# Cross-attention with a quantised feed-forward on one core: feed-forward clamps on GpSimd, roundings and transposes spread over each unit, finer extremes, small blocks at both ends, padding zeroed by VectorE

## The chip, the cores and the metric

The kernel runs on one core of one Trainium2 chip. The metric is the device time in microseconds, the median of several runs; lower is better. Profiles are one execution each, taken by the hardware profiler. In them PE is TensorE, DVE is VectorE, ACT is ScalarE, POOL is GpSimd and SP is SyncE, which here only issues DMAs.

## The reference

The inputs are x (32 x 100 x 256), a context (32 x 361 x 256) and one mask, all float32. The output is x after two residual steps.

```
x = x + attention(layernorm(x), ctx, ctx, WQ, WK, WV, WO, mask)    # 16 heads of 64
x = x + ffn(layernorm(x), W1, b1, W2, b2)                          # 256 -> 1024 -> 256

def affine_quantize(x):
    scale = max((max(x) - min(x)) / 255, 1e-8)       # over the whole tensor
    zp = clip(round(-min(x) / scale) - 128, -128, 127)
    q = clip(round(x / scale) + zp, -128, 127)

def qlinear(x, W, b):
    xq, sx, zx = affine_quantize(x)
    wq, sw = sym_quantize(W)
    return einsum("bsh,oh->bso", xq - zx, wq) * (sx * sw) + b

ffn(x) = qlinear(gelu(qlinear(x, W1, b1)), W2, b2)
```

What matters for the order of work is that each of the two quantised layers needs the largest and the smallest value of its whole input before its first element can be rounded. So there are two points at which everything must be known: the normalised x of all 3200 rows before the first layer, and all 3200 x 1024 GELU outputs before the second.

## The kernel before

*Attention* goes through the 32 batches in turn. For each it makes scores of 16 heads, exponentials on ScalarE, transposed weights, the product with the values, and keys and values of the next batch. The order on TensorE is written out by hand there; in the feed-forward a scheduler orders TensorE by priority and data, and `follow(a, b)` pins an instruction behind another on one engine.

At the start the context is loaded into three buffers `c`, whose columns 361 to 384 are padding that must be zero (L170 to L171, on GpSimd). The values of batch 0 (`v_part`, L276) read this padding in their third slice. After them TensorE transposes the normalised x of the first group (`ln1_T`, L325), which waits for `ln1` (L309, VectorE), and that for the inverse deviations (L299, L300, GpSimd). GpSimd also builds the identity there, loads two biases (L582, L583) and copies a constant (L541).

`residual` (L515) adds each batch's attention output, keeps running extremes, and `keep` (L122) writes the row with the second bias to a DRAM buffer `xb2`, from which the feed-forward reads it back into 128-row blocks. `normalize` (L129) makes the normalised x in place.

*Feed-forward, first layer.* The eight groups of four batches (400 rows each) are rounded to int16 (`ix`), clamped into bf16 (`xq`), transposed on TensorE (`turn`, L746) and copied by ScalarE (`xqT`, L749). `round_rows` (L722) does rounding and clamp through `to_integers` (L699), whose two parts are

```
done = nc.vector.tensor_scalar(i, src, r, None, ALU.mult)   # L705, or on ScalarE, L707
return nc.vector.tensor_scalar(dst, i, lo, hi, ALU.max, ALU.min)   # L710
```

The groups form units of 1, 1, 2, 2 and 2 groups. A unit has eight slices `fc` of the hidden width; for each TensorE multiplies (L781) and ScalarE applies GELU (L788) into `h`. VectorE takes the maximum and minimum of `h` over `spans` of slices (L794, L795): 2, 2, 4 in the first unit, 4 and 4 in the others. The groups of the next unit are rounded and turned together at the third slice of the unit before it.

`affine_params` (L99) reduces the extremes over the partitions on GpSimd (L107) and makes scale, inverse scale `rs`, zero point and bounds on VectorE (L109 to L119).

*Second layer.* The 25 blocks of 128 rows are grouped into `blocks` of 1, 3, 4, 4, 4, 4, 4 and 1. Each block is rounded in two halves (`ih`, ScalarE or VectorE), clamped by VectorE (`hq`), multiplied (L824), scaled and added to the kept row (`ot`, L831), and written (L834). The final sum of a block stands on VectorE just behind its clamps.

`warm` (L141) puts idle matmuls where TensorE would stand still.

Of the kernel before, what the change touches and what calls it, by code (L numbers as in the profile page):

```python
# [8 lines left out]
F32 = mybir.dt.float32  # L9
BF16 = mybir.dt.bfloat16  # L10
# [10 lines left out]
MAGIC = 12582912.0  # L21
# [6 lines left out]
def kernel(  # L28
# [66 lines left out]
    def follow(a, b):  # L95

        tc.add_manual_dep(a.ins, b.ins.name, ORDER)

    def affine_params(ext, name, weight):  # L99

        def col(n):
            return const.tile([P, 1], F32, tag=f"{n}{name}", name=f"{n}{name}")

        al = const.tile([P, 2], F32, tag=f"al{name}", name=f"al{name}")
        nc.gpsimd.partition_all_reduce(al, ext, P, bass_isa.ReduceOp.max)  # L107
        sc, rs, z, lo, hi = col("sc"), col("rs"), col("z"), col("lo"), col("hi")
        nc.vector.tensor_tensor(sc, al[:, 0:1], al[:, 1:2], ALU.add)  # L109
        nc.vector.tensor_scalar(sc, sc, 1.0 / 255.0, 1e-8, ALU.mult, ALU.max)  # L110
        nc.vector.reciprocal(rs, sc)


        nc.vector.tensor_scalar(z, al[:, 1:2], rs, MAGIC, ALU.mult, ALU.add)
        nc.vector.tensor_scalar(z, z, MAGIC, 0.0, ALU.subtract, ALU.max)
        nc.vector.tensor_scalar(lo, z, QMAX - QMIN, -1.0, ALU.min, ALU.mult)
        known = nc.vector.tensor_scalar(hi, lo, QMAX - QMIN, None, ALU.add)
        c = col("c")
        follow(nc.vector.tensor_tensor(c, sc, weight, ALU.mult), known)  # L119
        return rs, lo, hi, c, known, al  # L120

    def keep(b, adder, queue):  # L122

# [2 lines left out]
        queue.dma_start(out=xb2[b], in_=t)  # L126
        return i

    def normalize(b, after):  # L129

        xb = xg[b // G][:, b % G, :]
        i = nc.vector.tensor_scalar(
            xb, xb, mv2[:, b, 0:1], rstd2[:, b : b + 1], ALU.subtract, ALU.mult
        )
        follow(i, after)
# [5 lines left out]
    def warm(ps, n, gate=None):  # L141

        if gate is not None:
            nc.tensor.matmul(ps[: gate.shape[1], : gate.shape[1]], gate, gate, start=True, stop=True)
        for _ in range(n):
            nc.tensor.matmul(ps, idle[:, :P], idle, start=True, stop=True)


    with ExitStack() as att:
# [17 lines left out]
        NCB = 3  # L167
        cbuf = [wpool.tile([P, NDC, SP], F32, tag=f"c{i}", name=f"c{i}") for i in range(NCB)]
        pb = wpool.tile([TP, 2 * NHP, SP], F32, tag="p", name="p")
        for t in cbuf + [pb]:  # L170
            nc.gpsimd.memset(t[:, :, S:SP], 0.0)  # L171

        qbuf = [
            wpool.tile([P, PAIRS, G, 2, RH], F32, tag=f"q{q}", name=f"q{q}") for q in range(NQ)
# [501 lines left out]
    N = B * T  # L676
    h = hpool.tile([P, NFC, N], F32, tag="h", name="h")

    sizes = [1, 3] + [G] * ((N // P - 5) // G) + [1]
    blocks = [(sum(sizes[:i]), n) for i, n in enumerate(sizes)]  # L680
    assert sum(sizes) == N // P and len(blocks) == NG


    ext1 = const.tile([P, 2], F32, tag="ext1", name="ext1")
    with tc.high_priority():
        nc.vector.memset(ext1, -BIG)
        for r, op, neg, col in ((rmax, ALU.max, False, 0), (rmin, ALU.min, True, 1)):
            nc.vector.tensor_tensor(r, r, mv2[:, :, 0], ALU.subtract)
            nc.vector.tensor_tensor(r, r, rstd2, ALU.mult)
            found = nc.vector.tensor_reduce(ext1[:T, col : col + 1], r, AX.X, op, negate=neg)  # L690
        rx, lox, hix, c1, known, alx = affine_params(ext1, "x", scales["1"][1])
    warm(ps_h.tile([P, 512], F32, tag="ph", name="warm2"), 7, alx)

    def rows(dram, first, n):

        r = dram.rearrange("b t d -> (b t) d")[first * P : (first + n) * P]
        return r.rearrange("(c p) d -> p c d", p=P)

    def to_integers(pool, dst, src, r, lo, hi, tag, on_vector, after=None):  # L699

        i = pool.tile(list(src.shape), I16, tag=f"i{tag}", name=f"i{tag}") if tag[0] == "x" else (
            pool.tile([P, NF2, G * P], I16, tag=f"i{tag}", name=f"i{tag}")[:, :, : src.shape[2]]
        )
        if on_vector:
            done = nc.vector.tensor_scalar(i, src, r, None, ALU.mult)  # L705
        else:
            done = nc.scalar.activation(i, src, AF.Copy, bias=0.0, scale=r)  # L707
        if after is not None:
            follow(done, after)
        return nc.vector.tensor_scalar(dst, i, lo, hi, ALU.max, ALU.min)  # L710

    identb = const.tile([P, P], BF16, tag="identb", name="identb")
    nc.vector.tensor_copy(identb, ident)
# [2 lines left out]
    units = [(0, 1), (1, 1)] + [(g, 2) for g in range(2, NG, 2)]  # L716
    xqTs = {}
    gelu = None

    xqs = {}  # L720

    def round_rows(g, part, parts, on_vector, after):  # L722

        if part == 0:
            xqs[g] = f1.tile([T, G * D], BF16, tag="xq", name=f"xq{g}", bufs=4)
        src = xg[g].rearrange("t b d -> t (b d)")
        n = G // parts
        sl = slice(part * n * D, (part + 1) * n * D)
        done = to_integers(
            f1, xqs[g][:, sl], src[:, sl], rx[:T], lox[:T], hix[:T], f"x{n}", on_vector, after  # L730
        )
        if part == parts - 1 and g < len(blocks):

            nc.sync.dma_start(out=xf[g][:, : blocks[g][1], :], in_=rows(xb2, *blocks[g]))
        return done

    def turn(g, part, parts):

# [19 lines left out]
    k = 0  # L758


    done = round_rows(0, 0, 2, False, None)
    done = round_rows(0, 1, 2, True, done)
    for part in range(2):
        turn(0, part, 2)
    done = round_rows(1, 0, 1, True, done)
    follow(keep(B - 1, nc.vector, nc.sync), done)
    round_rows(2, 0, 1, True, done)
    for u, (g, n) in enumerate(units):
        ts = slice(g * GT, (g + n) * GT)
        spans = (2, 2, 4) if u == 0 else (4, 4)  # L770
        ends = [sum(spans[: i + 1]) for i in range(len(spans))]
        for fc in range(NFC):
            if fc == 2 and u + 1 < len(units):
                for i in range(*units[u + 1][:1], sum(units[u + 1])):
                    if i > 3:
                        round_rows(i, 0, 1, False, gelu)
                    turn(i, 0, 1)
            ph = ps_h.tile([P, 2, 512], F32, tag="ph", name=f"ph{u}_{fc}")
            for i in range(n):
                for dc in range(NDC):  # L780
                    nc.tensor.matmul(  # L781
                        ph[:, i, :GT],
                        w1qt[:, dc, fc * P : (fc + 1) * P],
                        xqTs[g + i][:, dc, :],
                        start=(dc == 0),
                        stop=(dc == NDC - 1),
                    )
            gelu = nc.scalar.activation(  # L788
                h[:, fc, ts].rearrange("p (k t) -> p k t", k=n), ph[:, :n, :GT],
                AF.Gelu, bias=b1t[:, fc : fc + 1], scale=c1,  # L790
            )
            if fc + 1 in ends:
                src = h[:, fc + 1 - spans[ends.index(fc + 1)] : fc + 1, ts]
                nc.vector.tensor_reduce(hmax[:, k : k + 1], src, AX.XY, ALU.max)  # L794
                done = nc.vector.tensor_reduce(hmin[:, k : k + 1], src, AX.XY, ALU.min)  # L795
                k += 1
                if k == 1:
                    round_rows(3, 0, 1, True, done)
        if u == 0:
            normalize(B - 1, done)  # L800

    ext2 = const.tile([P, 2], F32, tag="ext2", name="ext2")
    with tc.high_priority():
        nc.vector.tensor_reduce(ext2[:, 0:1], hmax[:, :k], AX.X, ALU.max)
        nc.vector.tensor_reduce(ext2[:, 1:2], hmin[:, :k], AX.X, ALU.min, negate=True)
        rh, loh, hih, c2, known, _ = affine_params(ext2, "h", scales["2"][1])
    warm(ps_h.tile([P, 512], F32, tag="ph", name="warm3"), 18, hmax[:, k - 1 : k])

    ff1.close()
    f2 = ctx.enter_context(tc.tile_pool(name="f2", bufs=2))  # L810
    for i, (first, n) in enumerate(blocks):
        hq = f2.tile([P, NFC, G * P], BF16, tag="hq", name=f"hq{i}", bufs=3)
        for k in range(2):
            sl = slice(k * NF2, (k + 1) * NF2)
            on_vector = k == 1 if n == 1 else k == 0 and i % 2 == 0
            to_integers(
                f2, hq[:, sl, : n * P], h[:, sl, first * P : (first + n) * P],
                rh, loh, hih, f"h{k}", on_vector, known if on_vector else None,
            )
        ot = f2.tile([P, G, D], F32, tag="ot", name=f"ot{i}")  # L820
        po = ps_h.tile([P, G, D], F32, tag="ph", name=f"pf{i}")
        for c in range(n):
            for fc in range(NFC):
                nc.tensor.matmul(  # L824
                    po[:, c, :],
                    hq[:, fc, c * P : (c + 1) * P],
                    w2qt[:, fc, :],
                    start=(fc == 0),
                    stop=(fc == NFC - 1),
                )  # L830
        nc.vector.scalar_tensor_tensor(  # L831
            ot[:, :n, :], po[:, :n, :], c2, xf[i][:, :n, :], ALU.mult, ALU.add
        )
        nc.sync.dma_start(out=rows(out, first, n), in_=ot[:, :n, :])  # L834


# [39 lines left out]
```

## Time and profile before

| | us |
|---|---|
| median of 3 runs | 1345.15 |
| lowest and highest run | 1345.11 and 1346.25 |
| the profiled execution, its own time | 1349.12 |
| span of its instructions | 1347.3 |
| mean granted clock of TensorE | 0.99 of full |

The profiled execution is 4.0 us above the median, so numbers from its rows are used for differences. Times in its rows count from the start of the span. A row of a timeline gives start, length, engine, line, operation, and in brackets how long the engine stood idle before it and what ended that. A group's row gives busy time and mean length of one instruction. The length of an instruction is up to 0.1 us more than the distance to the next one's start, because neighbours overlap.

### The profile page before, as it was taken

What the parts mean: (1) busy time and instruction counts of PE and PEld (TensorE: products, weight loads), DVE (VectorE), ACT (ScalarE), POOL (GpSimd) and SP (SyncE); (2) the same over time, 40 slices, a digit from 0 to 9 for tenths busy, and PEclk for the clock granted to TensorE, in tenths of its full rate; (3) what the DMA queues carried; (4) which work ended last, traced back from release to release, by engine and by line L of the source; (5) the groups of instructions that cost most, each with busy time, mean ns of one, the idle gap of its engine ahead of it and who ended that gap; (6) DMA issues with size and microseconds to landing.
All of it is one profiled execution on the core that took longest, in us unless ns stands there. A gap on an engine that the chain in (4) does not pass through costs nothing.

```text
span 1347.3 us, 25422 instructions
## 1 busy us (share of the span) xinstructions
PE 1308.6 (97%) x10064; PEld 809.2 (60%) x10064; DVE 784.7 (58%) x2377; ACT 693.2 (51%) x1918; POOL 86.7 (6%) x181
## 2 busy tenths in 40 slices
PE   8999999999999999999999999999999999999847
PEld 4666566666566566666566666665566666666416
DVE  4566455664366554664366653664466653575897
ACT  1556445564355455553355454553455553463845
POOL 1000000110011000110011000110011000110000
PEclk9999999999999999999999999999999999999979
DMA  8010001000000000000000000000000000000202
GB/s 260 12 43 12 11 12 39 23 16 3 12 19 18 12 12 1 19 19 12 12 18 19 12 3 11 18 19 12 11 19 18 13 1 12 10 11 4 82 20 99
DMA packets 24895, 33.02 MB, mean 25 GB/s; under 512 B 1788, under 2 KB 22852, under 8 KB 24775
## 3 DMA queue, kind: packets, MB, share of 16 engines
q1 hardware_dynamic: 21854, 24.91, 6.2%
q0 software_dynamic: 2096, 5.28, 1.3%
q8 instruction: 79, 1.29, 0.4%
q10 hardware_dynamic: 824, 1.19, 0.3%
q14 instruction: 42, 0.34, 0.1%
HBM read 24.82 MB, written 6.55 MB: 23 GB/s over the span
## 4 chain that ended last, share of the span: by engine, by line
PE 93%; issue 6%; DVE 1%; ACT 0%; POOL 0%; POOLq 0%; DVEq 0%
PE pv L276 25%; PE pk L245 23%; PE sc L412 13%; PE av L457 10%; PE pt L362 7%; PE pq L337 6%; PE py L494 6%; PE pf L824 2%; PE po L478 1%; PE po L508 0%; PE ptx L325 0%; DVE ot L831 0%; ACT p L393 0%; DVE ih L705 0%; DVE hq L710 0%
## 5 line engine op out<-in xcount | busy, mean ns | idle before, releaser
L276 PE MATMUL pv<-wvt,c 128*128 128x512 f32 x768 | 340.3, 599 | 3.0 <-POOL c L171 3.0
L245 PE MATMUL pk<-c,wkt 128*128 128x361 f32 x1016 | 314.2, 467 | 0.0
L252 ACT COPY kT<-pk 128x361 f32<-128x361 f32 x254 | 117.2, 462 | 365.8 <-PE pk L245 365.8
L393 ACT ACTIVATE p<-p,m 114x361 f32<-114x361 f32 x512 | 298.0, 596 | 7.8 <-DVE m L423 7.8
L245 PEld LDWEIGHTS pk<-c,wkt 128*128 128x128 f32 x1016 | 191.9, 190 | 113.2 <-issue 1.0
L423 DVE CUSTOM_DVE_ANT_0 p<-sc,maskt 114x361 f32<-114x361 f32 x512 | 252.3, 533 | 11.8 <-PE sc L412 6.9
L276 PEld LDWEIGHTS pv<-wvt,c 128*128 128x128 f32 x768 | 143.7, 191 | 176.6 <-issue 161.9
L374 DVE COPY pT<-pt 128x300 f32<-128x300 f32 x50 | 22.3, 469 | 351.5 <-PE pt L362 351.5
L412 PE MATMUL sc<-kT,q 64*114 64x361 f32 x1024 | 208.8, 490 | 0.0
L374 ACT COPY pT<-pt 128x300 f32<-128x300 f32 x462 | 169.0, 414 | 73.8 <-PE pt L362 71.2
L362 PEld LDWEIGHTS pt<-ident,p 50*128 50x128 f32 x3072 | 131.9, 139 | 77.4 <-issue 51.1
L438 DVE TENSOR_SCALAR p<-p,r 114x361 f32<-114x361 f32 x512 | 173.6, 404 | 2.6
L283 DVE COPY v<-pv 128x512 f32<-128x512 f32 x192 | 130.1, 683 | 29.2 <-PE pv L276 28.9
L457 PEld LDWEIGHTS av<-pT,v 128*64 128x64 f32 x3072 | 132.8, 137 | 18.5 <-ACT pT L374 15.0
L457 PE MATMUL av<-pT,v 128*64 128x100 f32 x3072 | 140.0, 250 | 0.0
L362 PE MATMUL pt<-ident,p 50*128 50x50 f32 x3072 | 133.9, 221 | 0.3 <-DVE p L438 0.3
L393 ACT ACTIVATION_READ_ACCUMULATOR p<-p,m 114x1 f32 x512 | 101.9, 199 | 0.0
L337 PE MATMUL pq<-xnT,wqt 128*128 128x400 f32 x256 | 87.9, 500 | 0.2 <-ACT xnT L328 0.2
L125 POOL TENSOR_TENSOR xb<-x,b2a 100x256 f32<-100x256 f32 x31 | 22.9, 738 | 900.2 <-DVE rmax L518 891.1
L412 PEld LDWEIGHTS sc<-kT,q 64*114 64x114 f32 x1024 | 77.1, 184 | 4.3 <-issue 0.6
L494 PE MATMUL py<-aT,wot 128*128 128x400 f32 x224 | 76.4, 499 | 0.0
L432 DVE RECIPROCAL r<-rsum 114x4 f32<-114x4 f32 (+1 forms) x131 | 22.9, 175 | 90.7 <-ACT p L393 90.7
(119 smaller groups left out, 710.1 us busy)
## 6 DMA issues: line engine op xcount, KB each, us to landing
c<-in_ctxT_dram SPq DMA_DIRECT2D x31, 361.0 KB, 3.0
x<-in_x_dram SPq DMA_DIRECT2D x8, 400.0 KB
xb<-xb POOLq DMA_DIRECT2D x31, 100.0 KB, 2.1
x<-xb SPq DMA_DIRECT2D x5, 512.0 KB, 4.0
out_dram<-ot SPq DMA_DIRECT2D x5, 512.0 KB, 2.9
wqt<-in_wq_dram SPq DMA_DIRECT2D x4, 256.0 KB
wot<-in_wo_dram SPq DMA_DIRECT2D x1, 1024.0 KB, 8.0
w<-in_w1T_dram POOLq DMA_DIRECT2D x1, 1024.0 KB, 5.5
```

What stands on the lines that cost most here:

```text
L245: nc.tensor.matmul(pk[:, :S], wkt[q][:, dc, col * P : (col + 1) * P], c[:, dc, :S], start=(dc == 0), stop=(dc == NDC - 1),)
L276: nc.tensor.matmul(pv[:SC, :], c[:, dc, s * SC : (s + 1) * SC], wvt[h][:, dc, :], start=(dc == 0), stop=(dc == NDC - 1),)
L283: return nc.vector.tensor_copy(vs[b, h][:, s, :], pv[:SC, :])
L337: nc.tensor.matmul(pq[:, :GT], wqt[q][:, dc, pair * P : (pair + 1) * P], xnTs[g][:, dc, :], start=(dc == 0), stop=(dc == NDC - 1),)
L362: nc.tensor.transpose(pts[k][:SC, (h * NSC + c) * TH : (h * NSC + c + 1) * TH], pb[ks, h0 + h, c * SC : (c + 1) * SC], ident[ks, ks],)
L374: copies.append(copy(pT[:, :, k, :], src))
L393: done = nc.scalar.activation(s, s, AF.Exp, bias=ms[h], scale=-1.0, accum_out=rsum[:, h : h + 1])
L412: nc.tensor.matmul(pss[h][:TP, :S], qbuf[pair // PAIRS][k * DK : (k + 1) * DK, pair % PAIRS, j, :, :].rearrange("p k t -> p (k t)")[:, :TP ...
L423: found = nc.vector.tensor_tensor_reduce(pb[:, h, :S], pss[h][:TP, :S], maskt, 1.0, BIG, ALU.add, ALU.min, ms[h])
L438: nc.vector.tensor_scalar(s, s, r[:, h : h + 1], None, ALU.mult)
L457: nc.tensor.matmul(av[k * DK : (k + 1) * DK, (pair - p0) * T : (pair - p0 + 1) * T], vs[b, pair // HP][:, c, h * DK : (h + 1) * DK], pTs[i ...
L494: nc.tensor.matmul(py[:, :GT], wot[:, c, dc * P : (dc + 1) * P], aT[:, c, :, :].rearrange("p j t -> p (j t)"), start=(c == 0), stop=(c == ...
```

## The change

1. VectorE zeroes the padding of the three `c` buffers; GpSimd keeps that of `p`.
2. `affine_params` rounds the zero point by an int16 column instead of two additions of a large constant, so one VectorE operation less stands before the bounds; bounds and the product `c` become separate steps that the caller places. The clamps use the constant -255 as lower bound instead of `lo`, so of the two bounds only `hi` is an operand.
3. Group 0's two roundings are both on ScalarE; their tiles are touched once before the ranges are known, by two small ScalarE copies and a one-column memset.
4. The first layer's clamps of groups 2 to 7 go to GpSimd, and so do the last row's bias sum, its store and its normalisation. Group 3's rounding goes from VectorE to ScalarE.
5. Roundings and transposes have places of their own inside the units (`rounded`, `turned`) instead of standing in pairs.
6. `spans` become 1, 1, 2, 4 in the first unit and 2, 2, 2, 2 in the third and fourth: 16 spans instead of 11.
7. After the last clamp GpSimd runs an all-reduce whose result is not used.
8. The second layer's blocks are 1, 2, 2, 4, 4, 4, 4, 2, 1, 1, with kept rows in seven places instead of eight; the final sum of a block stands two blocks later on VectorE; which halves VectorE rounds follows `halved`.
9. 5 instead of 7 warm matmuls stand before the first layer.

The diff, cut:

```diff
-        nc.vector.tensor_scalar(z, al[:, 1:2], rs, MAGIC, ALU.mult, ALU.add)
-        nc.vector.tensor_scalar(z, z, MAGIC, 0.0, ALU.subtract, ALU.max)
-        nc.vector.tensor_scalar(lo, z, QMAX - QMIN, -1.0, ALU.min, ALU.mult)
-        known = nc.vector.tensor_scalar(hi, lo, QMAX - QMIN, None, ALU.add)
+        def bounds(after=found):
+            i = nc.vector.tensor_scalar(z, al[:, 1:2], rs, QMAX - QMIN, ALU.mult, ALU.min)
+            follow(i, after)
+            nc.vector.tensor_scalar(lo, z, 0.0, -1.0, ALU.max, ALU.mult)
+            known = nc.vector.tensor_scalar(hi, lo, QMAX - QMIN, None, ALU.add)
+            return known
...
-        for t in cbuf + [pb]:
-            nc.gpsimd.memset(t[:, :, S:SP], 0.0)
+        for t in cbuf:
+            nc.vector.memset(t[:, :, S:SP], 0.0)
+        nc.gpsimd.memset(pb[:, :, S:SP], 0.0)
...
-    sizes = [1, 3] + [G] * ((N // P - 5) // G) + [1]
+    sizes = (1, 2, 2, 4, 4, 4, 4, 2, 1, 1)
+    halved = (0, 1, 2, 4, 9)
...
+        for t in i0:
+            nc.scalar.copy(t[:, 0:1], epst[:T])
+        follow(nc.vector.memset(xq0[:, 0:1], 0.0), extreme)
+        known = bounds()
+        scaled = product(known)
+    warm(ps_h.tile([P, 512], F32, tag="ph", name="warm2"), 5, alx)
...
+    def bound_rows(g, engine, after=None):
+        xqs[g] = f1.tile([T, G * D], BF16, tag="xq", name=f"xq{g}", bufs=4)
+        done = engine.tensor_scalar(
+            xqs[g], ixs[g], hix[:T], QMIN - QMAX, ALU.min, ALU.max
+        )
+        if after is not None:
+            follow(done, after)
+        bring_back(g)
+        return done
...
+    for part in range(2):
+        sl = slice(part * G * D // 2, (part + 1) * G * D // 2)
+        nc.scalar.activation(i0[part], src[:, sl], AF.Copy, bias=0.0, scale=rx[:T])
+        after, before = nc.vector.tensor_scalar(
+            xq0[:, sl], i0[part], QMIN - QMAX, hix[:T], ALU.max, ALU.min
+        ), after
+        follow(after, before)
         turn(0, part, 2)
-    done = round_rows(1, 0, 1, True, done)
-    follow(keep(B - 1, nc.vector, nc.sync), done)
-    round_rows(2, 0, 1, True, done)
+    bring_back(0)
+    after = round_rows(1, nc.vector, after)
+    after = bound_rows(1, nc.vector, after)
+    after = round_rows(2, nc.vector, after)
+
+    done = bound_rows(2, nc.gpsimd, reduced)
+    added = keep(B - 1, nc.gpsimd, nc.gpsimd)
+    follow(added, done)
+    normalize(B - 1, added, nc.gpsimd)
+
+    rounded = {(1, 3): 3, (2, 1): 4, (2, 3): 5, (3, 1): 6, (3, 3): 7}
+    turned = {(0, 2): 1, (1, 2): 2, (1, 7): 3, (2, 4): 4, (2, 6): 5, (3, 4): 6, (3, 6): 7}
     for u, (g, n) in enumerate(units):
-        spans = (2, 2, 4) if u == 0 else (4, 4)
+        spans = (1, 1, 2, 4) if u == 0 else (2,) * 4 if u in (2, 3) else (4, 4)
         for fc in range(NFC):
-            if fc == 2 and u + 1 < len(units):
-                for i in range(*units[u + 1][:1], sum(units[u + 1])):
-                    if i > 3:
-                        round_rows(i, 0, 1, False, gelu)
-                    turn(i, 0, 1)
+            if (u, fc) in turned:
+                turn(turned[u, fc], 0, 1)
...
+            if (u, fc) in rounded:
+                i = rounded[u, fc]
+                round_rows(i, nc.scalar, gelu)
+                bound_rows(i, nc.gpsimd)
+
+    g2 = small.tile([P, 1], F32, tag="g2", name="g2")
+    nc.gpsimd.tensor_copy(g2, epst)
+    nc.gpsimd.tensor_copy(g2[:T], xqs[NG - 1][:, 0:1])
+    nc.gpsimd.partition_all_reduce(g2, g2, P, bass_isa.ReduceOp.max)
...
         for k in range(2):
+            if k == 1 and i in halved:
+                done = nc.vector.tensor_scalar(t, h[:, sl, ts], rh, None, ALU.mult)
+                follow(done, after)
+                after = done
+            else:
+                nc.scalar.activation(t, h[:, sl, ts], AF.Copy, bias=0.0, scale=rh)
...
+        if i >= 2:
+            done = finish(i - 2)
+            follow(done, after)
+            after = done
```

## The prediction

> **What bounds the kernel now.** I read the page first, then the waits, then the timeline of the two places where TensorE is not busy: the first 23 us and the feed-forward after 1248 us.
>
> ```profile
> span 1347.3 us, 25422 instructions
> PE 1308.6 (97%) x10064; PEld 809.2 (60%) x10064; DVE 784.7 (58%) x2377; ACT 693.2 (51%) x1918; POOL 86.7 (6%) x181
> ...
> PE 93%; issue 6%; DVE 1%; ACT 0%; POOL 0%; POOLq 0%; DVEq 0%
> ```
>
> TensorE holds 93% of the chain, and the change leaves its attention order alone: between 23 us and 1248 us I expect no difference. What can move is the "issue" 6%: 11.4 us at the start and 64 us in the feed-forward.
>
> The start, from the timeline:
>
> ```profile
> 12.77 0.28 POOL masks.py:199 TENSOR_SCALAR_AFFINE_SELECT ident<-ident 128x128 f32<-128x128 f32 x1 [11.43 <-issue]
> 13.02 0.27 POOL L171 MEMSET c<- 128x46 f32 x3
> 13.20 8.83 PE L276 MATMUL pv<-wvt,c 128*128 128x512 f32 x16 [2.97 <-POOL c L171]
> 16.32 1.07 POOL L300 TENSOR_TENSOR rstd<-v,mhalf 100x4 f32<-100x4 f32 x1
> 18.36 1.05 DVE L309 TENSOR_SCALAR xn<-x,mv,rstd 100x256 f32<-100x256 f32 x3
> 21.87 0.85 PE L325 MATMUL ptx<-ident,xn 100*128 100x100 f32 x8
> ```
>
> GpSimd spends 11.43 us on nothing the profile shows before its first select, so the padding of the context (L171) comes only at 13.0, and TensorE stands 2.97 us for it. The next work that needs another chain, the transposes of xn, starts at 21.87, though xn was ready at 19.41. So there are 2.4 us to win here and not 3.
>
> The feed-forward, from the timeline of VectorE and TensorE:
>
> ```profile
> 1257.39 0.99 DVE L794 TENSOR_REDUCE hmax<-h 128x1 f32<-128x800 f32 x1
> 1259.19 0.75 DVE L705 TENSOR_SCALAR ix<-x,rsx 100x1024 int16<-100x1024 f32 x1
> 1287.26 1.00 DVE L710 TENSOR_SCALAR xq<-ix,lox,hix 100x1024 bf16<-100x1024 int16 x2
> 1311.91 3.49 DVE L795 TENSOR_REDUCE hmin<-h 128x1 f32<-128x3200 f32 x1
> 1315.30 0.17 DVE L804 TENSOR_REDUCE ext<-hmax 128x1 f32<-128x11 f32 x1
> 1318.37 1.03 PE L824 MATMUL pf<-w2qt,hq 128*128 128x256 bf16 x8 [0.81 <-DVE hq L710]
> 1320.78 21.44 PE L824 MATMUL pf<-w2qt,hq 128*128 128x256 bf16 x192 [1.38 <-DVE hq L710]
> 1341.39 1.90 DVE L831 SCALAR_TENSOR_TENSOR ot<-pf,ch,x 128x1024 f32<-128x1024 f32 x2 [2.21 <-PE pf L824]
> ```
>
> From 1253.3 to 1315.3 VectorE has no gap, while ScalarE is done with its GELUs at 1298: the first layer is bound by VectorE's extremes. Call their end X = 1315.30. After X the second layer is bound by TensorE (192 matmuls at 0.11), and the end is a chain: last `ot`, its write, about 1.4 us of closing.
>
> **The change, part by part.**
>
> *Padding on VectorE.* Three memsets (0.127 each on GpSimd; VectorE's row of a 128x256 memset is 0.27, so 0.1 each) fall near 1.2 us, where VectorE is idle until 11.97. The value groups then run on from 10.06: 16 matmuls at 0.43 end at 16.9 (wvt's ACT queue has moved 1.13 MB by 10 us, so its data are no bound). GpSimd loses 0.2 there and gains one 0.2 copy that the new order puts ahead of L300, so rstd and xn stand where they were: transposes at about 19.45 for 21.87, **−2.4**. What is late next is xn, and TensorE idles from 16.9 to 19.4, 2.5 us. That matters for the clock:
>
> ```profile
> 12.00:14.00 2.00, 0.80 (x2) 0.49 (x3) 2.00 (x8) 0.00 (x0) 1.23 (x13) 1.00 0.90 299
> 14.00:16.00 2.00, 2.00 (x4) 0.86 (x3) 1.54 (x4) 0.00 (x0) 1.96 (x13) 0.60 1.09 365
> 16.00:18.00 2.00, 2.00 (x3) 0.67 (x2) 0.57 (x2) 0.00 (x0) 1.40 (x3) 0.55 0.99 316
> 18.00:20.00 2.00, 2.00 (x6) 0.95 (x5) 2.00 (x6) 0.00 (x0) 0.00 (x0) 1.00 1.09 363
> ```
>
> (The column after POOL is the granted clock.) After the old gap the clock stood at half from 14.4 to 17.8. Three more drops, at 1273.9, 1284.2 and 1301.2, lie whole multiples of 3.413 us from it; the windows before the first two held 43% and 38% of TensorE work, and a window with 53% was followed by none. [...] the 3.4 us at half clock cost up to 1.7 us of TensorE-bound work: I take −0.9. [...]
>
> *The first layer.* Off VectorE go, start to start: the half rounding 0.52, clamp of group 2 0.53, rounding and clamp of group 3 0.66 + 0.46, clamps of 4 to 7 1.81, L125 0.34, L132 0.32: 4.6 us. Ten more reduces come in at 0.07 each (0.91 for 800 and 1.73 for 1600 elements give 1.03 ns an element and 0.07 to 0.09 fixed): +0.7. Were VectorE still without a gap, X would move by −3.9. It will not be. ScalarE takes both halves of group 0's rounding (0.62 behind the first 0.72), and one step less stands between rs and hi (0.19), so the first GELU moves from 1256.10 to about 1255.7. From there ScalarE's order is fixed: GELUs of 400 at 0.59, copies 0.75, roundings 1.1. GELU 3 of the first unit is done at 1258.75, GELU 7 at 1261.1; VectorE, emptied, reaches them at 1258.4 and 1260.7 and waits 0.5 and 0.55. In the second unit the copy of xqT3 stands ahead of the last GELU on ScalarE. It needs the rounding of group 3 (end 1265.3), the clamp on GpSimd, P, and eight transposes (0.52) with three handovers (0.45): 1266.3 + P. VectorE reaches that half unit at 1268.1.
>
> P is in no row. From the rows of GpSimd:
>
> ```profile
> L125 POOL TENSOR_TENSOR xb<-x,b2a 100x256 f32<-100x256 f32 x31 | 22.9, 738 | 900.2 <-DVE rmax L518 891.1 <-issue 8.9
> L165 POOL MEMSET maskt<- 114x361 f32 x1 | 0.4, 405 | 0.0
> masks.py:199 POOL TENSOR_SCALAR_AFFINE_SELECT ident<-ident 128x128 f32<-128x128 f32 x1 | 0.3, 284 | 11.4 <-issue 11.4
> ```
>
> With 0.24 fixed (L534, one element), the two-input add makes 1.95 ns an element: 2.2 us for 1024. The memset's 0.85 ns, and the select's less, make 1.1 at best. One input and two operations lie between: 1.5, ends 1.1 and 2.2. Then xqT3 is copied at 1267.8, the last GELU ends at 1269.1, VectorE waits to 1269.3 (1.2 us), and has 44.7 us left (3.46 + 27.7 + 13.56) without further waits, since ScalarE's two-group units need 11.3 us against VectorE's 13.8: X = 1314.0, **−1.3**. P of 1.1 and 2.2 make −1.7 and −0.6.
>
> [...] so I keep both ends and −1.2. The last row's add, store and normalise follow on GpSimd (0.74 + 0.64 + 0.7) and are done by 1264, before group 3's clamp is ready; group 7's rounding comes 20 us later. SP loses that store and issues seven reloads instead of eight. Two fewer warm matmuls end before the first transpose anyway. [...]
>
> *The second layer.* Blocks are 1, 2, 2, 4, 4, 4, 4, 2, 1, 1 instead of 1, 3, 4 x5, 1. First matmul: the bounds lose one 0.19 step, about −0.1. I followed both engines with the rows' spacings (2048 wide: ScalarE 1.90, VectorE 1.19, clamp 0.72; 1024: 1.06, 0.66, 0.46; 512: 0.62, 0.40, 0.33). The old gap of 1.4 behind the first block becomes 0.6, but block 3 is rounded wholly on ScalarE (3.8 us) and TensorE waits about 1.0 for its second half. Last matmul: X + 26.4 for X + 26.9. The tail gains more: before, the 512 KB and 128 KB writes moved together from 1343.5 to 1345.5 (X + 30.2); now the last `ot` (256 wide, 0.48) ends near X + 27.1, with 128 KB behind it, moved by X + 28.4. Together **−1.8**. Two more SP issues at 0.37 find SP waiting.
>
> Sum: −0.9 − 1.2 − 1.8 = −3.9 (with no drop of the clock −5.4). The profiled execution took 1349.12 (span 1347.3), 4.0 above the median of the runs; differences are carried to the median: 1345.15 − 3.9 = 1341.2.
>
> **The rivals.** About 0.2% (2.7 us) is what a measurement of this kernel tells from no change.
> - No drop of the clock after the opening gap: 1339.7. [...] Chance 0.30; the forecast with the drop 0.45.
> - ScalarE and GpSimd give back the first layer [...], or the opening gap loses more: −1 to −2.6, 1343.5. For it: no row shows this clamp. Chance 0.18.
> - Slower: GpSimd becomes the bound of the first layer. Six clamps in series with the roundings and copies give X = 1294.6 + 6P, which passes the old X at P = 3.45, and passes all the other gains at about 4.0; at 5 us X is 1324.6 and the time 1351.8. Against it: that is twice the price of the two-input add. For it: `pow` on GpSimd takes 0.58 for one element, so not every operation runs at the add's pace, and int16 input has no row. Chance 0.07.
>
> **How the numbers follow.** Range 1338.9 to 1343.8: from no drop with P of 1.1 to the third case. Faster by over 0.2%: both first cases but for an edge, and a little of the third, 0.76; within 0.2%: 0.17; slower: 0.07.
>
> **What would show it.** Right: no wait of pv on c; ptx at 19.4; a half clock within 17 to 24 us; VectorE waiting on GELU for about 2 us before 1270 by the old clock and on nothing until X; a clamp row on GpSimd of 1.1 to 2.2 us; last `ot` at X + 27. Wrong: clamps over 3 us, hmax waiting on h in the two-group units, a TensorE gap over 1.5 us after the first block, or attention steps that moved.

## The result, and the profile after

| | before | after |
|---|---|---|
| median of 8 runs, us | 1345.68 | 1341.59 |
| lowest and highest run | 1345.11 and 1346.25 | 1341.12 and 1342.09 |
| the profiled execution, its own time | 1349.12 | 1342.09 |

The changed kernel is faster by 4.1 us; the ratio is 0.997, with a 95% interval of 0.9959 to 0.9981. The forecast was 1341.2, a gain of 3.9. The sum came out. Its first term did not, and another made up for it, so that the sum lies this close is in part luck.

The page of the changed kernel, its span, its busy times and its chain:

```profile
span 1340.3 us, 25456 instructions
PE 1308.5 (98%) x10060; PEld 809.4 (60%) x10062; DVE 778.5 (58%) x2385; ACT 696.2 (52%) x1926; POOL 96.3 (7%) x190
...
PE 93%; issue 3%; ACT 3%; POOL 0%; DMA 0%; DVE 0%; POOLq 0%; ACTq 0%
```

TensorE is busy as long as before, to 0.1 us. "issue" fell from 6% of the chain to 3%, but ScalarE rose from 0% to 3%: VectorE now waits for GELUs, so the chain is followed back through ScalarE. These shares are no saving. Now the three stages. The start, from the timeline:

```profile
1.11 0.21 DVE L181 MEMSET c<- 128x46 f32 x3
8.05 10.46 PE L287 MATMUL pv<-wvt,c 128*128 128x512 f32 x24
11.20 0.28 POOL masks.py:199 TENSOR_SCALAR_AFFINE_SELECT ident<-ident 128x128 f32<-128x128 f32 x1 [9.87 <-issue]
14.69 1.07 POOL L311 TENSOR_TENSOR rstd<-v,mhalf 100x4 f32<-100x4 f32 x1
16.72 1.05 DVE L320 TENSOR_SCALAR xn<-x,mv,rstd 100x256 f32<-100x256 f32 x3
18.35 0.85 PE L336 MATMUL ptx<-ident,xn 100*128 100x100 f32 x8
```

The padding no longer waits for GpSimd, and the 24 value matmuls run without a gap. But GpSimd's 11.43 us ahead of its select, which set the start of before, are 9.87 here, though nothing of the change stands ahead of that select on GpSimd. xn is ready at 17.77 instead of 19.41, and TensorE never waits for it. So the two openings differ by 3.5 us (21.87 to 18.35), while the two medians differ by 4.1 in all. Part of the 3.5 must be the execution and not the kernel.

The first layer, from the timelines of VectorE, GpSimd and ScalarE:

```profile
1253.04 0.57 DVE L838 TENSOR_REDUCE hmax<-h 128x1 f32<-128x400 f32 x1 [0.39 <-ACT h L832]
1255.49 0.98 DVE L838 TENSOR_REDUCE hmax<-h 128x1 f32<-128x800 f32 x1 [0.46 <-ACT h L832]
1257.87 1.82 DVE L838 TENSOR_REDUCE hmax<-h 128x1 f32<-128x1600 f32 x1 [0.50 <-ACT h L832]
1265.49 1.82 DVE L838 TENSOR_REDUCE hmax<-h 128x1 f32<-128x1600 f32 x1 [0.63 <-ACT h L832]
1262.00 1.11 POOL L752 TENSOR_SCALAR xq<-ix,hix 100x1024 bf16<-100x1024 int16 x1 [2.27 <-ACT ix L738]
1264.05 0.83 ACT L780 COPY xqT<-pty 128x800 bf16<-128x800 bf16 x1 [0.42 <-PE pty L777]
1310.15 0.17 DVE L854 TENSOR_REDUCE ext<-hmax 128x1 f32<-128x16 f32 x1
```

VectorE, which had no gap before, waits four times for GELU, 1.98 us in all, and then for nothing until X. The forecast named the last three of them, with 0.5, 0.55 and 1.2; the first, 0.39, it did not have. The clamp on GpSimd takes 1.11 us; it had been taken at 1.5.

The second layer, from the timelines of TensorE and VectorE:

```profile
1313.19 1.03 PE L901 MATMUL pf<-w2qt,hq 128*128 128x256 bf16 x8 [0.41 <-DVE hq L893]
1314.42 4.10 PE L901 MATMUL pf<-w2qt,hq 128*128 128x256 bf16 x36 [0.20 <-ACT ih L888]
1319.14 17.20 PE L901 MATMUL pf<-w2qt,hq 128*128 128x256 bf16 x156 [0.61 <-DVE hq L893]
1336.38 0.48 DVE L869 SCALAR_TENSOR_TENSOR ot<-pf,ch,x 128x256 f32<-128x256 f32 x1 [0.22 <-PE pf L901]
```

Of the 1.38 us behind the first block 0.20 are left (forecast 0.6); 0.61 are new, ahead of block 3's second half, whose rounding ScalarE had not done (forecast about 1.0). The last matmul ends at X + 26.2 and the last `ot` at X + 26.7; before it was X + 26.9 and X + 28.0.

### The profile page after: what moved, and what is told of

Same layout as the page of the kernel before. It is cut to its first block, busy times and chain, and to the rows that moved or that the text cites. A ratio compares the mean times of both kernels' runs of the same rounds, so it can differ in the third digit from the quotient of the medians.

```text
span 1340.3 us, 25456 instructions
## 1 busy us (share of the span) xinstructions
PE 1308.5 (98%) x10060; PEld 809.4 (60%) x10062; DVE 778.5 (58%) x2385; ACT 696.2 (52%) x1926; POOL 96.3 (7%) x190
## 4 chain that ended last, share of the span: by engine, by line
PE 93%; issue 3%; ACT 3%; POOL 0%; DMA 0%; DVE 0%; POOLq 0%; ACTq 0%
PE pv L287 25%; PE pk L256 23%; PE sc L423 13%; PE av L468 10%; PE pt L373 7%; PE pq L348 6%; PE py L505 6%; ACT h L832 1%; PE pf L901 1%; PE po L489 1%; ACT ih L888 0%; PE po L519 0%; PE ptx L336 0%; ACT ix L738 0%; DMA wkt<-in_wk_dram 0%
## 5 line engine op out<-in xcount | busy, mean ns | idle before, releaser
L468 PEld LDWEIGHTS av<-pT,v 128*64 128x64 f32 x3072 | 132.8, 137 | 18.5 <-ACT pT L385 15.0
```

The costliest lines, as they stand in the source:

```text
L468: nc.tensor.matmul(av[k * DK : (k + 1) * DK, (pair - p0) * T : (pair - p0 + 1) * T], vs[b, pair // HP][:, c, h * DK : (h + 1) * DK], pTs[i ...
```

## The experiments

Names with b are the kernel before with an edit, names with a the changed kernel with an edit. Each was timed beside the kernel before, whose medians were 1345.70, 1345.88 and 1345.95 us in the three sets, and each left one profiled execution. Since most effects are near 1 us, two tables taken from those executions carry the readings. A row of a table is one execution, so it tells which wait stood where, and the medians tell what it was worth. The 95% intervals of the medians against the kernel before are ±0.9 to ±1.7 us wide, so a difference near 1 us is shown by median and trace together, not by the median alone.

### The padding alone, and all but the padding

b_pad:

```diff
-        for t in cbuf + [pb]:
-            nc.gpsimd.memset(t[:, :, S:SP], 0.0)
+        for t in cbuf:
+            nc.vector.memset(t[:, :, S:SP], 0.0)
+        nc.gpsimd.memset(pb[:, :, S:SP], 0.0)
```

> The kernel before, with one part of the change alone: the padding of the three context buffers is written by VectorE. The prediction's sum (a new TensorE gap of about 2.5 us before the transposes of xn, and the half clock behind it): -0.9 us. Without the drop of the clock: -2.4. If the whole difference of the two profiled executions at 1248 us belongs to this part: -3.5. [...]

Measured: 1345.78, +0.1 against the kernel before (ratio 0.9992 to 1.0008).

a_nopad, the same lines the other way round:

> The changed kernel with the padding of the context buffers back on GpSimd, all else as changed. By the prediction's sum it loses 0.9 of the gain and stays 3.0 below the kernel before; if the opening is worth 3.5, it loses nearly all of it and stays only about 0.6 below. pv should wait about 3 us on the padding again[...].

Measured: 1342.17, 3.5 below the kernel before. a_again is the changed kernel itself.

> The changed kernel once more, beside the others: 4.1 us below the kernel before, as measured. Its profile shows a second opening: by the prediction a TensorE gap before the transposes of xn of up to 2.5 us; by the first profiled execution none.

Measured: 1341.78. So the padding is worth 0.4 us by this pair and nothing by b_pad. The interval of b_pad (−1.1 to +1.1 us) excludes the readings of 2.4 and 3.5 us. It does not exclude 0.9, but the TensorE gap and the half clock behind it, from which the 0.9 was made, stand in no trace. A reading of 0, by which rstd and xn still set the opening, has the number right for another reason than it gives: xn is ready in b_pad at 17.28, before TensorE asks for it at 18.27.

b_late and a_late put back what the profiled execution of before had shown, a late GpSimd:

```diff
+        nc.gpsimd.memset(pb[:, :5, :], 0.0)    # ahead of GpSimd's padding memsets
```

> The kernel before with a memset of 1920 elements (1.65 us by the rows of GpSimd's memsets) ahead of the padding, so that the padding comes at about 13.0, [...] and rstd and xn come as much later. If that late padding, with the half clock behind its gap, is what put that execution 3.4 above the median: transposes of xn at about 21.5, +3.4 against the kernel before. If the half clock was chance: transposes at 20.0, +2.0. If rstd and xn set the opening: +1.4.

> The changed kernel with the same memset ahead of GpSimd's own memsets. The padding doesn't wait for it, rstd and xn do: xn from about 17.4 to 19.0, so TensorE waits for xn and the time is +1.2 to +1.6 against the changed kernel, up to 1.7 more with a half clock behind the wait. By the prediction's opening term (-0.9 with, -2.4 without the half clock, sized on such a late execution) it lies 4.6 to 6.1 below b_late; if the padding is worth nothing even then, 3.9.

Measured: b_late 1347.11, +1.2 against the kernel before; a_late 1341.82, the time of the changed kernel. The two lie 5.3 apart, where the kernels without the late GpSimd lie 4.1 apart, so with GpSimd about 1.7 us late the padding is worth about 1.2 more than without. Both expectations missed in part: a_late should have lost 1.2 to 1.6, and b_late's 1.2 is nearest to the reading that rstd and xn set the opening, though in its trace TensorE waits for the padding.

The openings of ten executions (us; "full clock from" is the first entry of the trace's record of the granted clock, on the span's time):

| kernel | GpSimd idle ahead of the select | TensorE's wait for `c` | full clock from | xn ready | transposes |
|---|---|---|---|---|---|
| before | 11.43 | 2.97 | 4.2, half 14.4 to 17.8 | 19.41 | 21.87 |
| b_newl2 | 9.40 | 0.26 | 4.2 | 17.56 | 18.14 |
| a_nopad | 9.74 | 1.20 | 4.2 | 17.92 | 18.47 |
| b_late | 9.28 | 2.44 | 4.1 | 18.88 | 19.66 |
| after | 9.87 | none | 6.6 | 17.77 | 18.35 |
| b_pad | 9.17 | none | 6.7 | 17.28 | 18.27 |
| a_again | 9.47 | none | 5.7 | 17.58 | 17.75 |
| a_vclamp | 9.08 | none | 4.8 | 17.59 | 17.35 |
| a_dup2 | 9.76 | none | 7.0 | 17.90 | 18.43 |
| a_late | 8.88 | none | 5.1 | 18.43 | 17.57 |

The four executions left out (a_spans, a_dup2f, a_dup4, a_swap) have 9.1 to 9.7 ahead of the select, full clock from 4.9, 6.5, 7.0 and 6.5, and transposes at 17.8 to 18.4.

Three things are to be read here. First, the 11.43 us stand alone: the others are 8.9 to 9.9. The profiled execution of before also took longer than every one of the 101 runs of that kernel over all sets (the highest is 1346.68). Its opening is 3.4 to 3.7 us later than in a_nopad and b_newl2, and it stood 3.4 above the median of 1345.68: the excess is the opening. Against a_nopad, half of it is GpSimd (11.43 for 9.74), half the clock behind the gap (16 value matmuls in 8.83 us for 7.13). The lines of a_nopad, an ordinary execution with the padding on GpSimd, beside those of b_late:

```profile
6.71 3.60 PE L287 MATMUL pv<-wvt,c 128*128 128x512 f32 x8
11.32 0.27 POOL L181 MEMSET c<- 128x46 f32 x3
11.50 7.13 PE L287 MATMUL pv<-wvt,c 128*128 128x512 f32 x16 [1.20 <-POOL c L181]
```

```profile
12.51 0.26 POOL L172 MEMSET c<- 128x46 f32 x3
12.69 7.13 PE L277 MATMUL pv<-wvt,c 128*128 128x512 f32 x16 [2.44 <-POOL c L172]
```

The stall to be removed is 0.3 to 1.2 us, not 3. And the 16 matmuls behind it take 7.13 us, as in a_nopad, where before's took 8.83: even behind b_late's 2.44 no half clock follows. It came in one execution of the four that had a gap.

Second, without the wait the opening is not shorter by the wait. Where the record's first entry, at full clock, stands only at 6.6 or later, some of the key matmuls run slowly, up to 967 to 971 ns for 467. The tile `pk` in a_nopad and in after (min, median and max ns):

```profile
L270 PE MATMUL pk<-c,wkt x8: 467/467/571, 4.2 to 6.4; 128*128 128x361 f32 x8
```

```profile
L270 PE MATMUL pk<-c,wkt x8: 467/508/967, 4.5 to 7.8; 128*128 128x361 f32 x8
```

In the second the four that start before 6.6 take 967, 808, 808 and 548 ns, the four behind them 467 or 468. The clock column of the page shows 1.00 there, since its record begins only later. The rise varied from 4.1 to 7.0 over all profiled executions, though the first idle matmul stands at 1.2 in each. This moves the transposes of the kernels with VectorE's padding between 17.35 and 18.44: by and large, the later the rise, the later they stand. With the padding on GpSimd and no late GpSimd they stand at 18.14 and 18.47. So the padding gains about 1 us where the rise is early, and about nothing where it is late.

Why the rise is early or late is open. All four executions with the padding on GpSimd have it at 4.07 to 4.24, and all ten with the padding on VectorE later, at 4.82 to 7.04. If the order had no part in it, the four lowest of fourteen would be these four in 1 of 1001 cases. So it may be that the padding on VectorE itself brings the late rise and loses there what it gains at the wait; no run separates the two, and no trace shows how it would. If it is chance, a late rise in the old order would be covered by the wait for `c`, which no execution shows either.

Third, xn, the work said to be late next, is ready before the value matmuls end in eight of the ten rows. In a_late its last part comes 0.7 us after their end (17.73), and the median does not move, since TensorE begins with the batches that are ready and loses 0.25:

```profile
16.44 0.74 DVE L321 TENSOR_SCALAR xn<-x,mv,rstd 100x256 f32<-100x256 f32 x2 [1.23 <-POOL rstd L312]
17.57 0.34 PE L337 MATMUL ptx<-ident,xn 100*128 100x100 f32 x2
17.70 0.73 DVE L321 TENSOR_SCALAR xn<-x,mv,rstd 100x256 f32<-100x256 f32 x2
18.16 0.97 PE L337 MATMUL ptx<-ident,xn 100*128 100x100 f32 x6 [0.25 <-DVE xn L321]
```

### The second layer alone

b_newl2 is the kernel before with the new loop of the second layer:

```diff
-    sizes = [1, 3] + [G] * ((N // P - 5) // G) + [1]
+    sizes = (1, 2, 2, 4, 4, 4, 4, 2, 1, 1)
+    halved = (0, 1, 2, 4, 9)
...
-        nc.vector.scalar_tensor_tensor(
-            ot[:, :n, :], po[:, :n, :], c2, xf[i][:, :n, :], ALU.mult, ALU.add
-        )
+        if i >= 2:
+            done = finish(i - 2)
```

> The kernel before with the second layer of the change alone: blocks of 1, 2, 2, 4, 4, 4, 4, 2, 1, 1, their halved roundings, the residual adds one block later. By the prediction's sum -1.7 (its -1.8 less 0.1 for the bounds, which stay as before); last matmul at X + 26.5, data moved by X + 28.5. If the blocks only moved the waits about: 0. If the smaller first blocks make TensorE wait more than they save: slower, by up to 1.

Measured: 1344.16, -1.5 (ratio 0.9982 to 0.9995). Its profile has the last matmul at X + 26.4 and the end of the span at X + 30.5, 1.5 earlier than that of before. The term is right.

The second table holds lengths (us): from the all-reduce of the first ranges (`alx`) to the first GELU and to X, and from X to the last matmul and to the end of the span. From the first weight load for the transposes of xn to `alx` it is 1229.8 or 1229.9 in all rows but a_late (1230.5, with the wait inside its transposes): attention did not move.

| kernel | alx to first GELU | alx to X | X to last matmul | X to end |
|---|---|---|---|---|
| before | 4.87 | 64.07 | 26.92 | 32.0 |
| b_pad | 4.86 | 64.71 | 26.90 | 32.0 |
| b_late | 4.88 | 64.78 | 26.90 | 32.0 |
| b_newl2 | 4.86 | 64.07 | 26.38 | 30.5 |
| after | 4.57 | 62.40 | 26.20 | 30.2 |
| a_nopad | 4.56 | 61.99 | 26.20 | 30.4 |
| a_again | 4.57 | 62.58 | 26.19 | 30.2 |
| a_late | 4.29 | 61.72 | 26.20 | 29.9 |
| a_vclamp | 4.57 | 63.57 | 26.57 | 30.9 |
| a_spans | 4.57 | 62.86 | 26.22 | 30.6 |
| a_dup2 | 4.59 | 62.20 | 26.21 | 30.3 |
| a_dup2f | 4.59 | 63.60 | 26.20 | 30.3 |
| a_dup4 | 4.57 | 69.89 | 26.19 | 30.6 |
| a_swap | 4.56 | 61.92 | 26.20 | 30.3 |

The first layer of before is 64.4 us in the mean of its four rows, that of after 62.3 in the mean of after, a_nopad and a_again: -2.1 (-2.2 with a_late, whose feed-forward is the same). The second layer is -1.8 in the mean.

The clock moves these rows too. b_pad, b_late, after and a_again have a stretch of half clock between 1261 and 1267; before, b_newl2, a_nopad and a_late have none there. With it the layer goes from 64.75 to 62.5, without it from 64.07 to 61.9. Like against like, the change is worth about 2.2 either way. The fourth wait of the changed kernel, 0.63 above, is 0.30 in a_nopad, whose clock is full there:

```profile
1265.21 1.82 DVE L838 TENSOR_REDUCE hmax<-h 128x1 f32<-128x1600 f32 x1 [0.30 <-ACT h L832]
```

### The first layer taken apart

a_vclamp:

```diff
-                bound_rows(i, nc.gpsimd)
+                    done = bound_rows(i, nc.vector, done)   # between hmax and hmin
...
-    done = bound_rows(2, nc.gpsimd, reduced)
+    after = bound_rows(2, nc.vector, after)
```

> The changed kernel with the clamps of groups 2 to 7 on VectorE (that of group 2 behind its rounding, the others between the maximum and the minimum of the unit they are made in), all else as changed. If taking them off VectorE is what moved X: five clamps at 0.41 in its gapless stretch, and 0.2 to 0.4 for the later xqT3, +2.1 to +2.5 against the changed kernel. If VectorE's waits on GELU already hide them: 0 to +0.5.

Measured: 1343.55, +1.9 against the changed kernel (from 1341.67, the median of a_dup2 in the same set, which has that kernel's time). X came only 1.2 later than in the mean, and 1.6 later than in a_nopad, whose clock is full in that stretch as it is here. The added work first ate the wait of 0.39 and the fourth one (0.30 to 0.63), which the expectation had not taken off. Another 0.7 came behind X. Of this 0.4 stand before the first matmul, where VectorE's first rounding begins 0.46 after `rs`, for 0.1 in the changed kernel; why is open.

a_spans:

```diff
-        spans = (1, 1, 2, 4) if u == 0 else (2,) * 4 if u in (2, 3) else (4, 4)
+        spans = (2, 2, 4) if u == 0 else (4, 4)
```

> The changed kernel with the extremes by four chunks again (2, 2, 4 in the first unit, 4 and 4 in all others), so eight reduces of 1600 in the third and fourth unit become four of 3200, and two of 400 become none. If the finer spans keep VectorE from waiting for four GELUs at the head of the third unit: +1.2 to +1.4. If VectorE is bound by its own work: -0.7, ten reduces of 0.07 fixed cost less.

Measured: 1342.98, +1.3 (from the same 1341.67). X lies 0.9 later than in a_nopad; neither has half clock in that stretch. Its waits are 1.4 longer in all, and the ten reduces less save about 0.7 by the forecast's 0.07 each. The largest wait is at the head of the third unit, in the timeline of VectorE:

```profile
1269.35 3.49 DVE L838 TENSOR_REDUCE hmax<-h 128x1 f32<-128x3200 f32 x1 [1.24 <-ACT h L832]
```

The kernel before has this wait too, in two of four executions; of b_pad:

```profile
1270.68 3.48 DVE L795 TENSOR_REDUCE hmax<-h 128x1 f32<-128x3200 f32 x1 [0.54 <-ACT h L789]
```

The granted clock of b_pad is half from 1262.8 to 1266.2, in the middle of the matmuls that feed these GELUs, and that of b_late from 1263.6 to 1267.0; the two executions without the wait have full clock there. So the layer of these two is 64.7 and 64.8, not 64.1. The profile that the forecast was made from did not show it.

### The price of a clamp on GpSimd

a_dup2 and a_dup4 issue each clamp two and four times:

```diff
+        for _ in range(2 if engine is nc.gpsimd else 1):    # 4 in a_dup4
             done = engine.tensor_scalar(
                 xqs[g], ixs[g], hix[:T], QMIN - QMAX, ALU.min, ALU.max
             )
```

> The changed kernel with each of the six clamps on GpSimd issued twice, so 2.2 us for 1.1. The prediction's chain (rounding of group 3, clamp, transposes, copy of xqT3, last GELU of the second unit): X later by the whole 1.1 us. If VectorE has slack there: 0 to +0.5. If all six clamps were in series with the path: +6.6.

Measured: 1341.67, X unmoved, with 2.3 us for two clamps in the rows. The order on ScalarE tells why: with the longer clamp the scheduler had put the copy of xqT3 behind the last GELU of the second unit, not ahead of it. a_dup2f holds it ahead:

```diff
+            if (u, fc) == (1, 7):
+                follow(gelu, copied)
```

> The changed kernel with each clamp on GpSimd issued twice, and ScalarE's order held as in the changed kernel: the copy of xqT3 ahead of the last GELU of the second unit (doubling alone had let the scheduler put it behind). By the prediction's chain with that order: X +1.1. If the order makes no difference: 0, as with the doubling alone.

Measured: 1342.84, +1.0 against a_late of its set, which has the changed kernel's time; X +1.3. VectorE's wait in a_dup2, at the third unit, and in a_dup2f, in the second:

```profile
1268.84 1.82 DVE L839 TENSOR_REDUCE hmax<-h 128x1 f32<-128x1600 f32 x1 [0.48 <-ACT h L833]
```

```profile
1266.44 1.82 DVE L842 TENSOR_REDUCE hmax<-h 128x1 f32<-128x1600 f32 x1 [1.88 <-ACT h L834]
```

1.88 for 0.63 is what the doubled clamp adds. The chain of the prediction is right for the order that it assumed, and that order was not fixed.

> The changed kernel with each of the six clamps issued four times, 4.4 us. The slower rival of the prediction, X = 1294.6 + 6P on the clock of the profile before, against its measured end with 1.1 us: +7.4 (followed by hand through ScalarE and GpSimd +8.6), slower than the kernel before by 3 to 4.5. If GpSimd is only late once, for group 3: +3.3, still faster than before. hmax should then wait on h in the two-group units.

Measured: 1349.32, +3.4 against the kernel before and +7.7 against the changed one. VectorE waits 3.76, 1.11 and 3.12 for GELU, at the heads of the three two-group units:

```profile
1272.12 1.82 DVE L839 TENSOR_REDUCE hmax<-h 128x1 f32<-128x1600 f32 x1 [3.76 <-ACT h L833]
1287.14 1.82 DVE L839 TENSOR_REDUCE hmax<-h 128x1 f32<-128x1600 f32 x1 [1.11 <-ACT h L833]
1304.16 3.49 DVE L839 TENSOR_REDUCE hmax<-h 128x1 f32<-128x3200 f32 x1 [3.12 <-ACT h L833]
```

GpSimd's clamps stand on the path here, as the slower rival said; stretches of half clock, which this trace has more of than the others (mean granted clock 0.986, 0.990 to 0.995 in the others), are in the waits too. Four clamps took 4.73 us in the rows, for which the rival's formula makes X +9.3; measured +7.5. It has the place right and the size too high by a quarter.

a_swap has the exchange that a_dup2 had made by itself, with single clamps:

```diff
-    turned = {(0, 2): 1, (1, 2): 2, (1, 7): 3, (2, 4): 4, ...
+    turned = {(0, 2): 1, (1, 2): 2, (2, 0): 3, (2, 4): 4, ...
```

> The changed kernel with one exchange on ScalarE: the last GELU of the second unit ahead of the copy of xqT3. The wait of 0.3 to 0.6 us that VectorE has there goes; the third unit starts about 0.7 later, and VectorE comes to it 0.5 after its second GELU: X -0.3 to -0.6 against the changed kernel. If the third unit's start becomes the bound: 0.

Measured: 1341.53, 4.4 below the kernel before, against 4.1 for the changed kernel: the lowest median of all, but the intervals (0.9955 to 0.9980 here) do not part the two. X is 61.92 behind `alx`, against 62.40 and 62.58 in after and a_again, whose half clocks stand at the same places; the forecast was 0.3 to 0.6 less. The wait of 0.63 is gone and one of 0.18 stands at the third unit.

## Why the prediction was right in its sum, and where not

| step | predicted | measured | from |
|---|---|---|---|
| opening | -0.9 | +0.1 and -0.4 | b_pad, a_nopad |
| first layer | -1.2 | -2.1 | second table |
| second layer and tail | -1.8 | -1.5 alone, -1.8 in the table | b_newl2 |
| sum | -3.9 | -4.1 | medians |

**The opening failed.** The step was "transposes at about 19.45 for 21.87", with the working that rstd and xn stand where they were. Both ends came from one execution whose GpSimd was about 1.7 us later than in the others. The text had the warning and passed over it: that execution stood 4.0 above the median, and "differences are carried to the median". The excess sat in the very stall that the step removes. In ordinary executions the transposes stand at 18.1 to 18.5 before and 17.4 to 18.4 after. The TensorE gap of 2.5 us and the half clock behind it did not come, for two reasons. Without the late GpSimd xn is ready earlier. And the step let the transposes wait for all four batches of xn, where TensorE starts with the first: in a_late, with GpSimd held back, all of xn is ready only at 18.43, and the transposes start at 17.57 and lose 0.25. The working also ended the value matmuls at 16.9, which needs the early rise of the clock that its one trace had; with VectorE's padding they ended at 17.5 to 18.6. The -0.9 set a half clock of 3.4 us, up to 1.7 us of work, against the 2.4; that it would follow the new gap was an estimate of mine, which the one trace did not show. So -0.9 was nearer than -2.4 for a reason that was not the right one. The rival of 1339.7, which rested on the same 2.4, falls for the same reason.

**The first layer was right in mechanism and too small.** The three waits stand where they were put, nothing waits after 1270, and ScalarE's order sets them. The term missed 0.9. In its own sum, -3.9 and the three waits make -1.65, not the -1.3 of the text; the 0.39 of the first wait, which it did not name, is of that size. About 0.4 of the miss is P: with 1.1 the text's own sum makes -1.7. I had taken 1.5, between the paces of the memset (0.85 ns an element) and of the two-input add (1.95) on the same engine. The rows show 1.10 to 1.11: less the 0.24 fixed, that is an estimate of 0.85 ns for each of 1024 elements, the memset's pace. The rest, about 0.5, is not taken apart in full. Part of it is that the mean of before holds two executions with half clock and the forecast was made from one without; but the gain is about 2.2 between executions without it too. There the fourth wait is 0.30 and 0.31 (a_nopad, a_late), where the text with P of 1.1 leaves about 0.8: the copy of xqT3 starts 15.9 and 15.6 us behind `alx`, and 16.2 by the text. That a P of 2.2 would cost 1.1 more than one of 1.1 held in the order that the text assumed (a_dup2f, X +1.3), and not in the one that the scheduler then made (a_dup2).

How long GpSimd stands idle between the all-reduce and its first clamp was an estimate too, and turned the first layer's -1.3 into -1.2. In before's trace it stands idle 5.82 us ahead of L543, 8.9 ahead of L125 and 9.1 ahead of L299, which the profile puts to "issue"; why is not shown. Ahead of the clamp of group 2 it stood idle 7.43 us here, and this was not on the path: the clamp of group 2 ended at 1256.65 and its transposes began at 1256.71, but the copy behind them had its place on ScalarE only at 1258.86.

**The second layer was right.** Last matmul X + 26.2 for X + 26.4, last `ot` X + 26.7 for X + 27.1, the tail -1.8 for -1.8.

**The rivals.** That ScalarE and GpSimd give the first layer back is excluded by X. That GpSimd becomes the bound is real at four times the price (a_dup4, +3.4). At twice the price it costs nothing or 1.0 us, by the order on ScalarE, and stays faster than before, so the break-even lies between; with the formula's slope of 6 from the measured point an estimate is 4.2, for 4.0 in the text.

## What to carry to other kernels

If the profiled execution stands well above the median, find where the excess sits before a saving is read from it: here it was the very stall to be removed, and a second execution would have shown it. Where a scheduler orders an engine, a dependence followed by hand holds only for the order assumed, so a longer instruction may cost nothing, or more. Work taken off a bound engine is worth what is left after the waits that it uncovers, and those can be listed from the next engine's row ahead of time.

## What the runs showed of the hardware that I had not expected

- TensorE's first full clock came between 4.1 and 7.0 us, though the first matmul stands at 1.2 in all 14 executions, and a late one cost the kernels with VectorE's padding about 1 us. The four executions of the old order lie within 0.2 of each other (4.07 to 4.24), the ten of the new one spread over 2.2 (4.82 to 7.04); why stays open. Before the first entry of its record the profile shows 1.00, so the spacing of the matmuls has to be read.
- No share of TensorE work in a window separates those with a drop behind them from those without, counted in steps of 3.413 us from the first rise; five half-clock stretches in the records of before and after have just this length. In before the gap of the opening left 35% and a drop followed; b_late's left 47% and none did. But windows of 51% (b_pad, 1259.37 to 1262.78) and 55% (after, 1249.06 to 1252.47) were followed by half clock, and one of 43% (a_dup2, 1334.76 to 1338.18) was not. What decides it is open. The windows that the prediction puts at 43% and 38% are 41% and 35% by their rows.
- A VectorE multiplication of the mask (114x361, SBUF to SBUF) took 0.32 us (0.40 in a_dup4) in the executions where GpSimd's 16 small memsets were over, and 1.24 and 1.20 in before and b_late, where they ran beside it; it ended 0.2 us after the last memset. Why the two go together is open; no run tests it. It was not on the path.
